# Graph attention, second layer: the output scaling and part of the weight sums on VectorE, the shift of a normalisation on ScalarE

## Chip, core and metric

One core of a Trainium2 chip runs the whole program. Its engines are TensorE (PE in the profile, with PEld for its weight loads), VectorE (DVE), ScalarE (ACT), GpSimd (POOL) and SyncE (SP, which only issues DMAs). The metric is the device time of one execution in microseconds (us), taken as the median of several executions. The profiled execution's "span" runs from its first to its last instruction.

## The reference, cut to what matters

Two layers over N = 4096 nodes of 512 features, with a residual and a normalisation after each. The change touches only the second:

```python
def _L1_gnn_ref(node_matrix, adjacency_matrix, Wks, Wqs, Wvs, Wo):
    eye = jnp.eye(n)
    adj = jnp.maximum(adjacency_matrix, eye)
    q = jnp.einsum('nd,hdk->hnk', node_matrix, Wqs)      # 8 heads of 64
    k = jnp.einsum('nd,hdk->hnk', node_matrix, Wks)
    v = jnp.einsum('nd,hdk->hnk', node_matrix, Wvs)
    scores = jnp.einsum('hqk,hmk->hqm', q, k) * kd ** (-0.5)
    scores = scores + IDENTITY_BIAS * eye - MASK_VAL * (1.0 - adj)
    att = jax.nn.softmax(scores, axis=-1)
    return jnp.einsum('hqm,hmk,hko->qo', att, v, Wo)

x = _layernorm(x + _L0_gnn_ref(x, adj, ...))
x = _layernorm(x + _L1_gnn_ref(x, adj, ...))
```

For each head and each query, the masked exponentials of 4096 scores are summed, multiplied with v, and divided by their sum.

## The kernel before

**Tiling of the second layer's attention.** Queries are cut into 8 groups g of 512 and heads into 4 couples m, which makes 32 pairs (g, m). For each pair the 4096 keys come in 32 blocks j of 128. One unit (g, m, j) is: `score`, four products of q and k on TensorE into a PSUM tile `s_ps` of 128 keys x (2 heads x 512 queries); the exponential in place on ScalarE (line 1559); the product with the mask on VectorE (line 1562), which reads `s_ps` and writes a tile `p` in SBUF, the weights; and `products`, four products of v and p on TensorE that are accumulated over j in `o_ps` (line 1614). There are three `s_ps` tiles, each used again as soon as line 1562 has read it, and 18 `p` tiles.

**Steps.** Three units make a step, so a pair has steps 0 to 9 with three units and a short step 10 with units 30 and 31. `step` (line 1727) writes this order into the queues: the scores of its units; in a short step also the sums and a projection for earlier pairs (below); the exponentials and masks; in a short step `close1` and `divide`; `add_up` for each unit; then the products of the step before; at the end `later.step()`. What is handed over with `later.at(k, ...)` in step s goes into the queues at the end of step s + k - 1, in the order in which it was handed over. Each engine then works through its own queue in that order, and each instruction waits for what it needs.

**The sums of the weights** (`add_up`, line 1566). The 32 weight tiles of a pair make 16 couples a, b (j = 2i and 2i + 1). Couple 0 starts `q_sum` on GpSimd (line 1578). Of the other fifteen, thirteen are first added into a by a DMA that accumulates (line 1595, issued by GpSimd) and then added to `q_sum` by GpSimd (line 1582). For two of them, i = 7 and i = 15, GpSimd adds both tiles to `q_sum`, without a DMA. The last pair has an order of its own for its couples 8 to 15; its couple 7 is like that of the others.

**The division** (`divide`, line 1636). In the short step of a pair, TensorE sums the `q_sum` of the pair before over partitions (line 1633). Reciprocals follow on VectorE (line 1656; one at the end of this short step, one at the end of the next pair's step 0), ScalarE copies them to all partitions (line 1648, into `r`), and at the end of step 4 `rest` (line 1650) multiplies the pair's output `o_sb` with `r` on GpSimd (line 1652), which gives `on`, the left operand of a later projection.

**The normalisation** (`close1`, line 1686). In the short steps from pair 5 on, one tile of 128 rows is projected with Wo (line 1678), added to the residual on VectorE (line 1689), and `normal_factors` (line 507) takes mean and variance on VectorE (lines 510 and 512) and then runs four instructions of one column on GpSimd: variance plus epsilon (514), power -1/2 (516), mean times this (518), times -1 (519). At the end of the next pair's step 2 ScalarE applies scale and shift (line 1694), and SyncE writes the rows out. The end of the last pair uses `factors` (line 1698), `shift` (1708) and `normalise` (1713), which split the same work between GpSimd and ScalarE.

Of the kernel before, what the change touches and what calls it, by code (L numbers as in the profile page):

```python
# [12 lines left out]
AF = mybir.ActivationFunctionType  # L13
ALU = mybir.AluOpType
# [415 lines left out]
def tile_gat_then_masked_attention(  # L430
# [16 lines left out]
    nc = tc.nc  # L447
# [59 lines left out]
    def normal_factors(y):  # L507

        st = small.tile([P, 6], F32, name="bn_st")
        nc.vector.bn_stats(st, y)  # L510
        mv = small.tile([P, 2], F32, name="bn_mv")
        nc.vector.bn_aggr(mv, st)
        ve = small.tile([P, 1], F32, name="bn_ve")
        nc.gpsimd.tensor_scalar(ve, mv[:, 1:2], EPS, None, op0=ALU.add)
        rs = small.tile([P, 1], F32, name="bn_rs")
        nc.gpsimd.tensor_tensor(rs, ve, minus_half, op=ALU.pow)
        nb = small.tile([P, 1], F32, name="bn_nb")
        nc.gpsimd.tensor_tensor(nb, mv[:, 0:1], rs, op=ALU.mult)
        nc.gpsimd.tensor_scalar(nb, nb, -1.0, None, op0=ALU.mult)
        return rs, nb  # L520
# [33 lines left out]
    later = Later()  # L554
# [18 lines left out]
    with tc.tile_pool(name="l0", bufs=NG) as l0, \  # L573
# [39 lines left out]
        def values(n, g):  # L613

            sup[n, g] = pools[n % 2][1].tile([P, GT, W0], F32, name="sup_t", bufs=NG)
            return sup[n, g]
# [34 lines left out]
        with tc.tile_pool(name="l0s", bufs=2) as sp:  # L651
# [32 lines left out]
            def factors(g, s4):  # L684

                t0, t1 = g * GT, (g + 1) * GT
                a = sp.tile([P, GT, H0], F32, name="aj")
                nc.scalar.activation(a, fs[g][:, 0], AF.Exp)
                dj[g] = l0.tile([P, GT, H0], F32, name="dj")
                nc.scalar.activation(dj[g], fs[g][:, 0], AF.Exp, scale=SLOPE - 1.0)  # L690
                fr = sp.tile([P, 2, H0, GT], F32, name="fr")
                src = fs[g][:, 1].rearrange("p t h -> p h t")
                nc.scalar.activation(fr[:, 0], src, AF.Copy)
                nc.scalar.activation(fr[:, 1], src, AF.Exp, scale=1.0 - SLOPE)
                flat = fs[g].rearrange("p k t h -> p k (t h)")
                nc.vector.tensor_reduce(span[:, g, 0:2], flat, AX.X, ALU.max)
                nc.vector.tensor_reduce(span[:, g, 2:4], flat, AX.X, ALU.min)
                s0 = values(0, g)
                nc.gpsimd.tensor_copy(s0[:, :, D0], a[:, :, 0])
                nc.gpsimd.tensor_copy(s4[:, 1:, :, D0], a[:, :, 1:].rearrange("p t h -> p h t"))  # L700
                for h in range(H0):
                    dst = s4[:, h] if h else s0
                    nc.gpsimd.tensor_tensor(dst[:, :, 0:D0], s4[:, h, :, 0:D0],
                                            a[:, :, h, None].to_broadcast([P, GT, D0]),
                                            op=ALU.mult)
                    nc.sync.dma_start(sup_d[h][:, t0:t1, :], dst)

                def rest():


                    n = 2 * H0 * GT
                    row = sp.tile([P, n], F32, name="fr_row")
                    nc.vector.transpose(row, fr.rearrange("p k h t -> p (k h t)"))
                    r0 = g * G % W
                    dst = fr_d[g * G // W][:, :, r0:r0 + G].rearrange(
                        "k h (t a r) -> a (k h) t r", a=NQ, r=SQ)
                    for q in range(NQ):
                        nc.sync.dma_start(dst[q], row[q * SQ:(q + 1) * SQ, :])
                if g + 1 < NG:
                    later.at(1, rest)  # L720
                else:
                    rest()
# [269 lines left out]
        with wait_by_tile("l0v", 2) as vp:  # L992
# [81 lines left out]
            def close(w, t):  # L1074
                i = w * WT + t
                y = agg_t[w][:, t].rearrange("p h d -> p (h d)")
                rs, nb = normal_factors(y)

                def normalise():
                    nc.scalar.activation(y, y, AF.Identity, bias=nb, scale=rs)  # L1080
                    nc.sync.dma_start(x1_d[i // GT][i % GT * P:(i % GT + 1) * P, :], y)
                later.at(5 if w + 1 < NW else 6, normalise)
# [22 lines left out]
    with wait_by_tile("l1", 1) as l1, wait_by_tile("l1a", 2) as lp, \  # L1105
# [3 lines left out]
        kt, vt, qt, at, mdt, pt, pw, q_sum, o_t, o_sb, on_t = ({} for _ in range(11))  # L1109
# [413 lines left out]
        with wait_by_tile("l1w", 2) as wp, wait_by_tile("l1o", 1, space=PSUM) as op:  # L1523
            NB = 3
            later = Later()
# [40 lines left out]
            def add_up(g, m, j):  # L1566

                if j % 2 == 0:  # L1570
                    return
                a, b = pt.pop((g, m, j - 1)), pt.pop((g, m, j))
                i, n = j // 2, NT // 2
                at_end = (g, m) == pairs[-1]

                def first():
                    q_sum[g, m] = wp.tile([P, HP, G], F32, name="q_sum")
                    nc.gpsimd.tensor_tensor(q_sum[g, m], a, b, op=ALU.add)

                def add(p):  # L1580
                    q = q_sum[g, m]
                    nc.gpsimd.tensor_tensor(q, q, p, op=ALU.add)  # L1582

                if i == 0:
                    later.at(1, first)
                elif at_end and i >= n - 5:
                    last_sum.extend((a, b))
                elif at_end and i >= n - 8:
                    later.at(2, lambda: nc.gpsimd.dma_start(a, b, accum_op=ALU.add))
                    in_pairs.append(a)  # L1590
                elif i % 8 == 7:
                    later.at(2, lambda: add(a))
                    later.at(3, lambda: add(b))
                else:
                    later.at(2, lambda: nc.gpsimd.dma_start(a, b, accum_op=ALU.add))  # L1595
                    later.at(5, lambda: add(a))
# [28 lines left out]
            def places():  # L1625

                return [(c, c // KD, slice(c // MA % 2 * GH, (c // MA % 2 + 1) * GH))
                        for c in range(0, P, MA)]
# [7 lines left out]
            def divide(g, m, s):  # L1636

                if m == 0:
                    on_t[g] = wp.tile([P, NP1, G], F32, name="on")
                n = index[g, m, 0] // NT  # L1640
                den = wp.tile([P, GH], F32, name="den_h", bufs=1)
                nc.scalar.activation(den, s[:, 0:GH], AF.Copy, accum_out=total[:, n:n + 1])
                rh = wp.tile([P, GH], F32, name="r_h", bufs=1)
                r = wp.tile([P, G], F32, name="r1", bufs=1)

                def spread(c, e, half):
                    for a in range(e * KD, (e + 1) * KD, MA):
                        nc.scalar.activation(r[a:a + MA, half], rh[c:c + MA, :], AF.Copy)  # L1648

                def rest():  # L1650
                    nc.scalar.activation(den, rh, AF.Copy, accum_out=most[:, n:n + 1])
                    nc.gpsimd.tensor_tensor(on_t[g][:, m, :], o_sb.pop((g, m)), r, op=ALU.mult)

                def invert(t):
                    a = slice(t * P, (t + 1) * P)
                    nc.vector.reciprocal(rh[:, a], den[:, a])

                for t in range(GH // P):
                    later.at(1 + t, lambda t=t: invert(t))
                for k, place in enumerate(places()):  # L1660
                    later.at(3 + k // 2, lambda place=place: spread(*place))
                later.at(6, rest)
# [23 lines left out]
            def close1(g, t, s, wait=4):  # L1686
                i = g * GT + t
                y = y_t.pop((g, t))
                nc.vector.tensor_tensor(y, y, s, op=ALU.add)

                rs, nb = normal_factors(y)

                def normalise():
                    nc.scalar.activation(y, y, AF.Identity, bias=nb, scale=rs)
                    nc.sync.dma_start(out[i * P:(i + 1) * P, :], y)
                later.at(wait, normalise)

            def factors(s):
                st = small.tile([P, 6], F32, name="bn_st")
# [8 lines left out]
            def shift(mv):  # L1708
                less = small.tile([P, 1], F32, name="bn_ve")
                nc.scalar.activation(less, mv[:, 0:1], AF.Copy, scale=-1.0)  # L1710
                return less
# [68 lines left out]
            y = y_t[tiles[-5]]  # L1780
# [16 lines left out]
            rs, nb = normal_factors(y)  # L1797
# [30 lines left out]
            mv, rs = by[3]  # L1828
# [41 lines left out]
```

## Time and profile before

| | |
|---|---|
| median of 3 runs (lowest, highest) | 3319.39 us (3316.53, 3320.89) |
| profiled execution, its own time | 3318.25 us |
| span of the profiled execution | 3316.3 us, granted clock 0.999 |
| VectorE busy, of the span | 2479.2 us (75%) |
| ScalarE busy | 1950.6 us (59%) |
| GpSimd busy | 2163.6 us (65%) |
| GpSimd busy from 2000 to 2200 us | 191.19 of 200 us |
| VectorE busy from 2000 to 2200 us | 138.29 of 200 us |
| ScalarE busy from 2000 to 2200 us | 121.31 of 200 us |
| weight additions of line 1582 on GpSimd | 535 records, 1367.4 us, 2556 ns each |
| scalings of line 1652 on GpSimd | 31, median 2258 ns |

The second layer's attention runs from about 1420 us to the end. A row of the timeline reads: start in us, length in us, engine, line, operation, names out<-in, shapes, number of instructions merged into the row, and in brackets the idle time of that engine just before it with what ended it. The length that the profile gives for an instruction on GpSimd can hold time in which it waited for an earlier one, or for a resource. Some records of a trace can be missing.

### The profile page before, as it was taken

How to read it: one execution, taken by the hardware profiler on the slowest of the kernel's cores; microseconds unless marked ns; L12 is line 12 of the kernel's file. 1: busy time of each engine (PE TensorE's matmuls, PEld its weight loads, DVE VectorE, ACT ScalarE, POOL GpSimd, SP SyncE). 2: the span in 40 equal slices, each digit the busy share in tenths (PEclk: the TensorE clock that was granted, in tenths of full speed). 3: DMA queues.
4: the chain of work that ended last, by engine and by line, in shares of the span. 5: the costliest groups of instructions: out<-in, count | busy, mean ns of one | idle time of the engine just before them, and what ended most of it. 6: DMA issues, size and time to landing. Idle time of an engine off the chain costs nothing.

```text
span 3316.3 us, 67188 instructions
## 1 busy us (share of the span) xinstructions
PE 3297.3 (99%) x27144; PEld 1963.8 (59%) x27144; DVE 2479.2 (75%) x3188; ACT 1950.6 (59%) x2449; POOL 2163.6 (65%) x1594
## 2 busy tenths in 40 slices
PE   9999999999999999999999999999999999999998
PEld 8899999999999777733333333333333333333333
DVE  6689899898999677467767666676766767666666
ACT  1367868878776310156656656566565656656554
POOL 6630040040030244389999999999999999999995
PEclk9999999999999999999999999999999999999999
DMA  8988796686532443499898988889889799898884
GB/s 191 230 198 189 212 189 169 150 182 147 138 93 59 109 147 120 163 217 207 192 211 222 229 196 193 210 189 256 205 192 212 189 209 251 190 211 193 203 204 116
DMA packets 398800, 612.04 MB, mean 185 GB/s; under 512 B 167632, under 2 KB 248528, under 8 KB 398480
## 3 DMA queue, kind: packets, MB, share of 16 engines
q0 software_dynamic: 97760, 259.55, 42.9%
q1 hardware_dynamic: 299280, 345.88, 33.6%
q8 instruction: 215, 3.52, 0.4%
q10 hardware_dynamic: 1440, 2.23, 0.3%
q14 instruction: 105, 0.86, 0.1%
HBM read 315.87 MB, written 109.25 MB: 128 GB/s over the span
## 4 chain that ended last, share of the span: by engine, by line
PE 94%; DMA 2%; POOL 2%; DVE 1%; issue 1%; ACT 0%; ACTq 0%; POOLq 0%; DVEq 0%
PE o_ps L1095 27%; PE o_ps L1614 25%; PE s_ps L1146 25%; PE o_ps L850 5%; PE s_ps L1678 3%; PE s_ps L1306 2%; PE s_ps L1256 2%; PE s_ps L1263 2%; DMA p<-p 2%; PE x_ps L1263 1%; PE x_ps L1256 1%; PE s_ps L1633 1%; POOL q_sum L1582 0%; PE s_ps L1302 0%; POOL p L1595 0%
## 5 line engine op out<-in xcount | busy, mean ns | idle before, releaser
L1582 POOL TENSOR_TENSOR q_sum<-q_sum,p 128x1024 f32<-128x1024 f32 x535 | 1367.4, 2556 | 65.2 <-DMA p<-p 39.8
L1562 DVE TENSOR_TENSOR p<-s_ps,adjT 128x1024 f32<-128x1024 f32 x896 | 1044.0, 1216 | 469.6 <-ACT s_ps L1559 439.2
L1559 ACT ACTIVATE s_ps<-s_ps 128x1024 f32<-128x1024 f32 x1021 | 967.2, 1007 | 597.7 <-PE s_ps L1146 597.5
L1146 PE MATMUL s_ps<-q_sb,k_sb 64*64 64x512 f32 x8192 | 943.5, 589 | 2.5 <-DVE p L1562 2.5
L1614 PE MATMUL o_ps<-p,v_sb 64*64 64x512 f32 x8192 | 943.9, 590 | 0.0
L1095 PE MATMUL o_ps<-sup_t,p 128*128 128x129 f32 x8192 | 915.5, 275 | 1.2 <-DVE p L646 1.2
L1095 PEld LDWEIGHTS o_ps<-sup_t,p 128*128 128x128 f32 x8192 | 915.1, 192 | 1.6 <-DVE p L646 1.4
L646 DVE SCALAR_TENSOR_TENSOR p<-fr_t,dj,az 128x1024 f32<-128x1024 f32 x512 | 650.0, 1284 | 65.7 <-PE o_ps L1095 36.8
L1146 PEld LDWEIGHTS s_ps<-q_sb,k_sb 64*64 64x64 f32 x8192 | 312.5, 133 | 569.5 <-issue 454.6
L1614 PEld LDWEIGHTS o_ps<-p,v_sb 64*64 64x64 f32 x8192 | 310.1, 133 | 570.8 <-issue 560.3
L630 ACT ACTIVATE z<-fr_t,f 128x1024 fp8e4<-128x1024 f32 x512 | 557.3, 1143 | 102.6 <-DVE az L641 102.3
L1595 POOL DMA_DIRECT2D p<-p x409 | 435.3, 1305 | 9.9 <-PE o_ps L1614 9.1
L1071 POOL DMA_DIRECT2D agg<-base_d x32 | 29.0, 1218 | 386.9 <-DMA sup_t<-sup_d 204.7
L591 POOL COPY seen<-token 128x1 f32<-128x1 f32 x24 | 10.9, 456 | 356.8 <-DVE token L589 356.8
L1562 DVE TENSOR_TENSOR p<-s_ps,md 128x1024 f32<-128x1024 f32 x128 | 150.7, 1217 | 67.0 <-ACT s_ps L1559 63.3
L641 DVE TENSOR_TENSOR az<-adjT,z 128x512 int32<-128x512 int32 x256 | 175.3, 685 | 3.3 <-ACT z L630 2.1
L606 ACT ACTIVATE adjT<-stage 128x1024 fp8e4<-128x1024 bf16 x128 | 130.9, 1052 | 16.8 <-DMA stage<-adj_d 16.8
L1678 PE MATMUL s_ps<-wo_sb,on 128*128 128x512 f32 x240 | 111.2, 605 | 0.0
L1648 ACT ACTIVATE r<-r_h 32x256 f32<-32x256 f32 x248 | 102.3, 412 | 2.9
L1057 ACT ACTIVATE agg<-o_ps,rinv 128x128 f32<-128x128 f32 x128 | 41.9, 369 | 70.1 <-DVE den L1050 48.8
L1330 ACT ACTIVATE v<-s_ps 128x256 f32<-128x256 f32 x28 | 10.7, 382 | 115.0 <-PE s_ps L1306 100.0
L1678 PEld LDWEIGHTS s_ps<-wo_sb,on 128*128 128x128 f32 x240 | 43.1, 189 | 56.6 <-issue 54.7
(295 smaller groups left out, 2236.5 us busy)
## 6 DMA issues: line engine op xcount, KB each, us to landing
p<-p POOLq DMA_DIRECT2D x412, 512.0 KB, 9.1
k_sb<-k_d SPq DMA_DIRECT2D x128, 512.0 KB
v_sb<-v_d SPq DMA_DIRECT2D x128, 512.0 KB
adj_d<-in_adj_dram POOLq DMA_DIRECT2D x32, 1024.0 KB, 11.1
sup_t<-sup_d SPq DMA_DIRECT2D x120, 258.0 KB
fr_t<-fr_d SPq DMA_DIRECT2D x16, 1024.0 KB
adjT_d<-adjT SPq DMA_DIRECT2D x32, 512.0 KB
adjT<-adjT_d SPq DMA_DIRECT2D x32, 512.0 KB
```

Source lines behind the costliest of these rows:

```text
L630: nc.scalar.activation(z[:, k, :], fr_t[w, h][:, 0, :], AF.Sign, bias=fs[j // GT][:, 0, (j + k) % GT, h:h + 1], saturate=False)
L641: nc.vector.tensor_tensor(az.bitcast(I32), adjT[w, j // CJ][:, j % CJ:j % CJ + 2, :].bitcast(I32), z.bitcast(I32), op=ALU.bitwise_and)
L646: nc.vector.scalar_tensor_tensor(p, fr[:, 1, :], dj[j // GT][:, j % GT, h:h + 1], az_t[w, h, j // 2][:, j % 2, :], op0=ALU.max, op1=ALU.mult)
L850: nc.tensor.matmul(out[:, t * HD:(t + 1) * HD], xb[:, c, t * P:(t + 1) * P], wb[:, c, :], start=not more and t == 0 and c == 0, stop=c == ...
L1095: nc.tensor.matmul(o[t // BK][:, t % BK, :], p[:, t * P:(t + 1) * P], s, start=(j == 0 and t % BK == 0), stop=(j == NT - 1), skip_group_ch ...
L1146: nc.tensor.matmul(s[c:c + MS, e, :], k[r, a + c:a + c + MS], qt[g, m][r, :], start=True, stop=True)
L1559: nc.scalar.activation(s, s, AF.Exp, scale=float(KD) ** -0.5)
L1562: nc.vector.tensor_tensor(p, s, keep[:, None, :].to_broadcast([P, HP, G]), op=ALU.mult)
L1582: nc.gpsimd.tensor_tensor(q, q, p, op=ALU.add)
L1595: later.at(2, lambda: nc.gpsimd.dma_start(a, b, accum_op=ALU.add))
L1614: nc.tensor.matmul(o[c, n, :], v[r, j % CH, c], p[r, e, :], start=(j == 0), stop=(j == NT - 1))
L1678: nc.tensor.matmul(s, on_t[g][:, m, t * P:(t + 1) * P], wo_sb[:, m, :], start=(m == 0 and not onto), stop=(m == NP1 - 1), skip_group_check ...
```

## The change

Three edits, all in the second layer's attention:

1. `add_up`: for the couples i = 7 and i = 15, b is added to a on VectorE, and GpSimd then adds a alone to `q_sum`. VectorE's addition is handed over for the step at whose end the first of GpSimd's two stood; the one that GpSimd keeps stands where its second was.
2. `rest` in `divide`: the product of `o_sb` and `r` goes from GpSimd to VectorE, at the same place.
3. `close1`: mean and variance by `factors` (two instructions of one column on GpSimd in place of four), and, when the tile is due, `shift` and `normalise` on ScalarE: minus the mean, this times the factor, and then the row-wise scale and shift, three instructions in place of one.

```diff
@@ add_up
                 elif i % 8 == 7:
-                    later.at(2, lambda: add(a))
-                    later.at(3, lambda: add(b))
+                    later.at(2, lambda: nc.vector.tensor_tensor(a, a, b, op=ALU.add))
+                    later.at(3, lambda: add(a))
@@ divide
                 def rest():
                     nc.scalar.activation(den, rh, AF.Copy, accum_out=most[:, n:n + 1])
-                    nc.gpsimd.tensor_tensor(on_t[g][:, m, :], o_sb.pop((g, m)), r, op=ALU.mult)
+                    nc.vector.tensor_tensor(on_t[g][:, m, :], o_sb.pop((g, m)), r, op=ALU.mult)
@@ close1
-                rs, nb = normal_factors(y)
-
-                def normalise():
-                    nc.scalar.activation(y, y, AF.Identity, bias=nb, scale=rs)
+                mv, rs = factors(y)
+
+                def close():
+                    normalise(y, y, shift(mv), rs)
                     nc.sync.dma_start(out[i * P:(i + 1) * P, :], y)
-                later.at(wait, normalise)
+                later.at(wait, close)
```

The functions that `close1` now calls stood in the kernel already:

```python
def factors(s):
    ...
    nc.gpsimd.tensor_scalar(rs, mv[:, 1:2], EPS, None, op0=ALU.add)
    nc.gpsimd.tensor_tensor(rs, rs, minus_half, op=ALU.pow)
    return mv, rs

def shift(mv):
    less = small.tile([P, 1], F32, name="bn_ve")
    nc.scalar.activation(less, mv[:, 0:1], AF.Copy, scale=-1.0)
    return less

def normalise(s, y, less, rs, meanwhile=None):
    nb = small.tile([P, 1], F32, name="bn_nb")
    nc.scalar.activation(nb, less, AF.Copy, scale=rs)
    ...
    nc.scalar.activation(y, s, AF.Identity, bias=nb, scale=rs)
```

In the queues of the changed kernel VectorE's new addition for i = 15 stands directly behind `o_sb` (line 1757) and the second reciprocal (line 1656) of the next pair's step 0, and in front of the three masks of its step 1. The one for i = 7 stands behind the masks of step 6, the scaling behind the masks of step 4. The order of TensorE's instructions is what it was.

## The prediction

> **What bounds the kernel now.** I read the page first, its part on busy times and the 40 slices.
>
> ```profile
> PE 3297.3 (99%) x27144; PEld 1963.8 (59%) x27144; DVE 2479.2 (75%) x3188; ACT 1950.6 (59%) x2449; POOL 2163.6 (65%) x1594
> ```
>
> TensorE is busy 99% of the span, at a granted clock of 0.999. A busy TensorE can still run below its pace, so next came TensorE's waits from 1400 us on, then the chain that ended last in order of time.
>
> ```profile
> PE s_ps L1146 <- DVE p L1562: 2.5, 4, 1.6
> ```
>
> ```profile
> 2325.33 0.57 PE s_ps L1633 x8
> 2325.90 3.63 PE s_ps L1678 x8
> ...
> 2384.63 0.57 PE s_ps L1633 x8
> ```
>
> The reader is to see a pace: one pair takes 59.30 us (2384.63 - 2325.33), and the timeline shows the same 59.29 to 59.30 for all pairs with a projection except three (59.89, 60.16, 59.71); of the pairs without one, three take 55.66 and one 57.45. The excess is 0.59 + 0.86 + 0.41 + 1.79 = 3.65 us. That is all a faster VectorE, ScalarE or GpSimd can win here: 0.11%. GpSimd's 95% (191 of 200 us) costs only this much. So what decides is whether the work that arrives on VectorE delays TensorE. Here the timeline of one pair's change to the next (short step, then steps 0, 1, 2):
>
> ```profile
> 2212.72 0.22 POOL L514 TENSOR_SCALAR bn_ve<-bn_mv 128x1 f32<-128x1 f32 x1 [1.16 <-DVE bn_mv L512]
> 2213.01 0.57 POOL L516 TENSOR_TENSOR bn_rs<-bn_ve,minus_half 128x1 f32<-128x1 f32 x1
> ...
> 2214.14 2.36 POOL L1582 TENSOR_TENSOR q_sum<-q_sum,p 128x1024 f32<-128x1024 f32 x1
> 2216.44 1.86 POOL L1595 DMA_DIRECT2D p<-p  x2
> 2217.66 7.93 POOL L1582 TENSOR_TENSOR q_sum<-q_sum,p 128x1024 f32<-128x1024 f32 x3
> ...
> 2219.12 0.68 DVE L1757 TENSOR_TENSOR o_sb<-o_sb,o_ps 128x512 f32<-128x512 f32 x1
> 2219.72 0.95 DVE L1656 RECIPROCAL r_h<-den_h 128x128 f32<-128x128 f32 x1
> 2220.58 3.42 DVE L1562 TENSOR_TENSOR p<-s_ps,adjT 128x1024 f32<-128x1024 f32 x3
> 2224.23 0.15 PEld L1146 LDWEIGHTS s_ps<-q_sb,k_sb 64*64 64x64 f32 x4 [0.28 <-DVE p L1562]
> ```
>
> VectorE has no idle time between 2219.12 and 2224.00 (2220.58 + 3.42): it is the late one. Its third mask ends at 2224.00 and the weight load that needs this `s_ps` tile (third unit of step 2) starts on schedule at 2224.23, so 0.23 us are left. How much later it may be is seen where VectorE once waited for a weight tile:
>
> ```profile
> 1956.77 1.90 PE L1146 MATMUL s_ps<-q_sb,k_sb 64*64 64x512 f32 x16
> 1957.76 2.46 DVE L1562 TENSOR_TENSOR p<-s_ps,adjT 128x1024 f32<-128x1024 f32 x2 [1.63 <-DMA p<-p]
> 1959.04 1.09 PE L1146 MATMUL s_ps<-q_sb,k_sb 64*64 64x512 f32 x8 [0.37 <-DVE p L1562]
> ```
>
> The third unit's load was due at 1958.06 (loads go every 0.43 us, one slot ahead of their products), came at 1959.04, 0.98 late, and the pair lost 0.59: 0.39 was absorbed. So a delay d of step 1's masks costs TensorE d - 0.23 - 0.39 = d - 0.62 us.
>
> [...] in the first layer:
>
> ```profile
> 36.24 5.13 POOL L883 TENSOR_TENSOR base<-base,bb 128x1024 f32<-128x1024 f32 x2
> 38.35 0.80 DVE L801 TENSOR_TENSOR p<-xT 128x512 f32<-128x512 f32 x1
> 39.19 2.74 DVE L803 TENSOR_TENSOR p<-p,xT 128x512 f32<-128x512 f32 x1
> ...
> 1189.41 2.35 POOL L1285 TENSOR_TENSOR k_sb<-k_sb,p 128x1024 f32<-128x1024 f32 x1 [6.36 <-DVE k_sb L1291]
> 1189.50 2.41 DVE L1215 TENSOR_TENSOR w_sk<-w_sk,adjT 128x128 f32<-128x128 f32 x1
> ```
>
> L803 usually takes 0.68 and L1215 0.28; here they end 0.6 and 0.15 after GpSimd does. L801 slipped in between two GpSimd instructions, L803 had to wait out the whole next one. The masks of line 1562 have one input in PSUM and show none of this (1216 ns beside a busy GpSimd). [...] the three additions from 2217.66 really begin when the two DMA issues are done (2218.30) and take 7.29/3 = 2.43 each.
>
> **The change part by part.**
>
> *GpSimd, removed per pair:* two additions (2 x 2.43), one scaling (2.26), two small instructions (0.57, from 2213.58 to 2214.14): 7.7 us. All of it lies beside TensorE, except the 3.65 us above, each of which follows a wait of VectorE for a weight tile that a late DMA or GpSimd held. I take all four as gone: -3.65.
>
> *ScalarE, added:* `shift` 0.19 and the factor 0.28 (rows of lines 1710 and 1715 at the end of the program), the row-wise part as before: about 0.5 us at the end of step 2. Step 3's exponentials, which start at most 0.15 late there now, start about 0.6 late; VectorE idles 1.8 us before step 3's masks. Cost nothing; without that cover at most 0.5 x 26 = 13 us.
>
> *Scaling on VectorE:* 0.68 us (two SBUF inputs, 128x512, as L801), behind step 4's masks, where VectorE idles 1.66 us and the third mask of the next step has about 0.74 + 0.39 to spare. A cover of 2.8 us: even behind a whole GpSimd addition (2.43 + 0.68) it costs 0.3. I take 0.
>
> *Addition for i = 7*, behind step 6's masks: 1.22 us (row of line 1602, two SBUF inputs, 1224 ns), same cover. It costs only if GpSimd has more than 1.6 us to go; bounds 0 and 0.85 per pair. I take 0, since GpSimd is then catching up between DMAs.
>
> *Addition for i = 15*, in front of step 1's masks: here is no cover. VectorE comes to it at 2220.58. Where is GpSimd? It is idle before line 514 (1.16 us), so its phase is tied to VectorE's mean, and what follows moves up by the 0.57 us of the two small instructions: addition to 2215.93, DMA issues to 2217.73, additions to 2220.16 and 2222.59. VectorE arrives 0.42 us after the second has begun, waits 2.0 us, adds 1.22, and the masks start 2222.59 + 1.15 - 2220.58 = 3.15 us late (1.15: two instructions in a row overlap by 0.07). Cost 3.15 - 0.62 = 2.53 us. What is queued behind it: three masks, for which the three score products of step 2 wait, and everything of TensorE behind these. Bounds: with no wait 1.15 - 0.62 = 0.53; with a whole addition to wait out 1.15 + 2.43 - 0.62 = 2.96.
>
> *Sum.* 26 changes with a normalisation (pairs 5 to 30): 26 x 2.53 = 65.8. Pairs 1 to 4, where nothing ties GpSimd: margin the same, wait taken as half an addition: 4 x 1.7 = 6.8. Pair 0 (no reciprocal) 1; the last pair, whose couple 7 meets a reciprocal, 1.5; its scaling ahead of the last sums on VectorE 0.5. Less 3.65: +72 us. The profiled execution is 1.1 us below the median, so 3319.4 + 72 = 3391 us.
>
> **Rivals.**
> 1. *The addition costs its own length only* (it slips in front of GpSimd's second addition, or does not block). For it: 0.42 us of phase is little, and a DMA issue that takes that much longer lets VectorE in first. Against: both phases hang on the same instruction, and pairs repeat to 0.02 us. Then 26 x 0.53 to 26 x 0.95, + 5, - 3.65: +15 to +26, about 3340 us.
> 2. *The other couple is exposed as well.* If GpSimd begins an addition just before VectorE reaches i = 7, 31 x up to 0.85 more, and the wait at i = 15 is a whole one: +84 to +110, about 3415 us. For it: fixed phases, all or nothing. Against: GpSimd has about 8 us of idle time per pair by then (2.6 now, 7.7 more, less its own waits behind VectorE), and by step 6 it waits for DMAs between additions.
> 3. *Not slower:* the relief of GpSimd decides. Place: weight tiles held by late DMAs in steps 6 to 9; price -3.65 us, so 3315.7. It decides if step 1's masks come less than 0.62 + 0.12 us late (3.65/31 = 0.12). For it: only GpSimd is near full. Against: 1.15 us of addition alone is more than 0.74.
>
> **How the numbers follow.** Chances: forecast 0.64 (3360 to 3412), rival 1 0.22 (3332 to 3350), rival 2 0.08, rival 3 0.06. Predicted 3391 us. The range 3338 to 3414 takes the forecast and most of rival 1 and leaves out most of rivals 2 and 3. Below 0.2% (6.6 us) this kernel cannot be told from unchanged: within it 0.05, nearly all of rival 3; faster 0.02, since only 3.65 us are there to be won; slower 0.93.
>
> **What would show it.** In the profile after: line 1592 on VectorE in two kinds, behind line 1656 lasting about 3.2 us with GpSimd's L1582 ending 1.2 us before it; TensorE waiting on `p` of L1562 once per pair in step 2; pairs of about 61.8 us; GpSimd busy near 170 of 200 us. A mean of 1.22 us for line 1592 there and pairs of 59.8 us are rival 1; pairs of 59.30 throughout are rival 3. I am wrong in the main step if masks of step 1 start late and TensorE does not wait.

## The result, and the profile after

| | before | after |
|---|---|---|
| median (lowest, highest), same chip | 3319.33 us (3316.53, 3320.89) | 3399.02 us (3393.62, 3401.53) |
| ratio, 95% interval | | 1.0238 [1.0228, 1.0248] |
| profiled execution: span, granted clock | 3316.3 us, 0.999 | 3397.5 us, 0.997 |

The change makes the kernel 79.7 us slower; 72 were forecast. The span grew by 81.2 us.

The page after, busy times:

```profile
PE 3330.9 (98%) x27144; PEld 1952.8 (57%) x27144; DVE 2667.4 (79%) x3282; ACT 1971.4 (58%) x2503; POOL 2007.8 (59%) x1446
```

GpSimd lost 156 us, VectorE gained 188, and TensorE has the same instructions as before. TensorE's waits from 1400 us on (line waited for, us in total, times, longest), and the busy times of a window in the middle (PE, PEld, DVE, ACT, POOL, then clock, DMA share, GB/s):

```profile
PE s_ps L1146 <- DVE p L1562: 44.8, 31, 1.7
```

```profile
2000.00:2200.00 200.00, 192.89 (x1704) 66.48 (x1700) 151.93 (x134) 122.19 (x167) 168.40 (x104) 1.00 0.80 187
```

The wait that stood at 2.5 us in 4 places has become 44.8 us in 31, about one for each change of pairs. GpSimd is at 168.4 of 200 us, from 191.2: relieved as planned, and to no use. These waits are 42.3 us more than before; TensorE's busy time is 33.6 us more (3330.9 - 3297.3) with as many instructions. The next view shows where most of both comes from.

The same stretch of a pair's change that the prediction read, now after (start, length, engine, line, operation):

```profile
2304.16 0.22 POOL L1704 TENSOR_SCALAR bn_rs<-bn_mv 128x1 f32<-128x1 f32 x1 [6.42 <-DVE bn_mv L1702]
...
2305.01 2.35 POOL L1582 TENSOR_TENSOR q_sum<-q_sum,p 128x1024 f32<-128x1024 f32 x1
...
2307.32 1.83 POOL L1595 DMA_DIRECT2D p<-p  x2
...
2308.52 5.47 POOL L1582 TENSOR_TENSOR q_sum<-q_sum,p 128x1024 f32<-128x1024 f32 x2
...
2310.56 0.68 DVE L1757 TENSOR_TENSOR o_sb<-o_sb,o_ps 128x512 f32<-128x512 f32 x1
2311.16 0.94 DVE L1656 RECIPROCAL r_h<-den_h 128x128 f32<-128x128 f32 x1
...
2312.02 3.05 DVE L1592 TENSOR_TENSOR p<-p,p 128x1024 f32<-128x1024 f32 x1
2313.95 3.33 POOL L1578 TENSOR_TENSOR q_sum<-p,p 128x1024 f32<-128x1024 f32 x1
2314.99 7.02 DVE L1562 TENSOR_TENSOR p<-s_ps,adjT 128x1024 f32<-128x1024 f32 x6
2316.26 3.35 PE L1146 MATMUL s_ps<-q_sb,k_sb 64*64 64x512 f32 x24 [1.70 <-DVE p L1562]
...
2317.39 0.21 PEld L1146 LDWEIGHTS s_ps<-q_sb,k_sb 64*64 64x64 f32 x8 [0.92 <-DVE p L1562]
...
2318.52 0.21 PEld L1146 LDWEIGHTS s_ps<-q_sb,k_sb 64*64 64x64 f32 x8 [0.93 <-DVE p L1562]
...
2319.43 2.75 PE L1614 MATMUL o_ps<-p,v_sb 64*64 64x512 f32 x24
```

Read it from GpSimd: the issues end at 2309.15 (2307.32 + 1.83), the two additions behind them at 2313.99. At 2.43 us each, the second began at 2311.56. VectorE came with line 1592 at 2312.02, 0.46 us too late, and ended 1.08 us after GpSimd's addition. So line 1592 lasts 3.05 us in place of 1.22, step 1's masks start 2.97 us late (2314.99 - 2312.02), and TensorE waits 1.70 us for the first of them. Its loads for the other two units then follow the masks, 1.13 us apart (2317.39, 2318.52), so that these 24 products last 3.35 us, where 24 others last 2.75. The 1.70 and the 0.60 make 2.30 of the 2.46 us that the pair loses. In turn line 1578 on GpSimd lasts 3.33 in place of 2.36: counted back from its end (2317.28), its 2.36 us began at 2314.92, near the end of VectorE's addition (2315.07).

In the groups of the window from 1400 us on (busy, mean ns, idle time before), line 1592 averages 2525 ns, more than twice its own length; GpSimd, by contrast, idles 161.9 us in sum ahead of the 31 normalisations:

```profile
L1592 DVE TENSOR_TENSOR p<-p,p 128x1024 f32<-128x1024 f32 x63 | 159.1, 2525 | 0.0
...
L1704 POOL TENSOR_SCALAR bn_rs<-bn_mv 128x1 f32<-128x1 f32 x31 | 6.9, 222 | 161.9 <-DVE bn_mv L1702 161.8
```

The starts of line 1633 give the period of each pair. Before: 59.30. After: 61.76 in most of the pairs with a projection, 62.4 to 62.6 in three, 63.9 in three, 61.92 in one and 60.07 in one. In the pair of 60.07, VectorE met GpSimd at another moment and the addition for couple 15 lasted 1.35 us.

The pairs of 63.9 have a cause of their own. The trace's record of TensorE's granted clock has it at one half from 2441.34, 2690.51 and 2939.69 us, for 3.413 us each time, and otherwise from 1400 us on only in the last 8 us; in the kernel before only in the last 7. The first two rows are the stretches of 3.41 us before and after the first of these moments; the other two lie around a stall whose clock stays whole (the first number behind the length is TensorE's busy time, the third from the right its clock):

```profile
2437.93:2441.34 3.41, 1.67 (x16) 0.41 (x16) 3.41 (x4) 0.74 (x2) 3.41 (x2) 1.00 0.43 123
2441.34:2444.75 3.41, 3.41 (x20) 1.00 (x16) 2.97 (x3) 2.06 (x3) 3.33 (x2) 0.50 0.02 5
2376.49:2379.90 3.41, 1.83 (x16) 0.42 (x16) 3.41 (x4) 0.74 (x2) 3.41 (x2) 1.00 0.32 93
2379.90:2383.31 3.41, 3.37 (x32) 1.13 (x32) 3.41 (x4) 3.01 (x6) 3.33 (x2) 1.00 0.02 5
```

The three moments lie 249.17 and 249.18 us apart, which is 73 times 3.413. In the run with couple 15 alone (below) they are 1879.64, 2251.69 and 2930.95: 372.05 and 679.26 us apart, 109 and 199 times 3.413. With both traces cut at these moments and at whole multiples of 3.413 us from them (from 1450 us to 20 us before the end), the stretches that come before a halving are, in the run with couple 15 alone, the three in which TensorE works least: 1.66, 1.67 and 1.69 us; the next has 1.70. In the kernel after they have about 1.67, 1.67 and 1.70, and two others, at 1.68 and 1.70, are not followed by a halving. So each of the six halvings comes behind a stretch in which TensorE worked 1.66 to 1.70 of 3.413 us; it comes in three pairs of 26, though TensorE waits 1.68 to 1.71 us at 25 of the 26 changes of pairs, and around the stall of the last two rows, where the stretch has 1.83 us of work, it does not. In run 7, where TensorE waits 0.92 us at a time, no stretch has less than 2.41, and the clock stays whole. This is a regularity of three traces; the cause of the halving was not shown.

In these three pairs couple 7 meets GpSimd as well, as in others:

```profile
2467.30 0.87 POOL L1595 DMA_DIRECT2D p<-p  x1 [0.69 <-PE o_ps L1614]
...
2467.91 8.40 POOL L1582 TENSOR_TENSOR q_sum<-q_sum,p 128x1024 f32<-128x1024 f32 x3
2467.97 3.67 DVE L1592 TENSOR_TENSOR p<-p,p 128x1024 f32<-128x1024 f32 x1
```

VectorE comes 0.20 us before the DMA issue ends (2468.17) and still waits out the first of the three additions behind it; run 8 comes back to this. Couple 7 lasts 3.5 to 3.75 us in 11 of 32 pairs and 1.2 to 2.7 in the others.

The sum of the prediction beside what the periods show (the normal periods taken, as there, as 59.30 and 55.66, so that the 3.65 us of before's late pairs are subtracted):

| term | forecast us | measured us |
|---|---|---|
| 26 changes of pairs, couple 15 | 65.8 | 64.0 (26 x 2.46) |
| further in these pairs | 0 | 7.0: clock 4.6 (3 x 1.52), couple 7 3.9 (six pairs at 0.61 to 0.79), other +0.2, the pair of 60.07 -1.7 |
| pairs 1 to 4 | 6.8 | 6.6 |
| up to the first line 1633 (pair 0) | 1 | 4.3 |
| the last pair and its end | 2 | 2.9 |
| before's late pairs | -3.65 | -3.65 |
| sum | 72 | 81.2 (span) |

The 4.3 us hold some scatter: in the run without either couple (below), where nothing ahead of that point is changed, the first line 1633 comes 1.8 us later than before. The share of 1.52 for a halved clock is from the run with couple 15 alone, where such pairs take 63.28.

### The profile page after: what moved, and what is told of

It reads as the page before. It is cut to its first block, busy times and chain, and to the rows that moved or that the text cites. A ratio compares the mean times of both kernels' runs of the same rounds, so it can differ in the third digit from the quotient of the medians.

```text
span 3397.5 us, 67150 instructions
## 1 busy us (share of the span) xinstructions
PE 3330.9 (98%) x27144; PEld 1952.8 (57%) x27144; DVE 2667.4 (79%) x3282; ACT 1971.4 (58%) x2503; POOL 2007.8 (59%) x1446
## 4 chain that ended last, share of the span: by engine, by line
PE 88%; DVE 6%; issue 4%; ACT 1%; POOL 0%; DMA 0%; DVEq 0%; ACTq 0%; POOLq 0%
PE o_ps L1095 27%; PE s_ps L1146 23%; PE o_ps L1614 22%; PE o_ps L850 5%; DVE p L1562 3%; PE s_ps L1678 3%; PE s_ps L1306 2%; PE s_ps L1256 2%; PE s_ps L1263 2%; PE x_ps L1263 1%; DVE p L1592 1%; ACT s_ps L1559 1%; PE x_ps L1256 1%; DVE o_sb L1757 1%; PE s_ps L1633 1%
## 5 line engine op out<-in xcount | busy, mean ns | idle before, releaser
L1562 DVE TENSOR_TENSOR p<-s_ps,adjT 128x1024 f32<-128x1024 f32 x896 | 1045.0, 1216 | 372.4 <-ACT s_ps L1559 359.6
L1582 POOL TENSOR_TENSOR q_sum<-q_sum,p 128x1024 f32<-128x1024 f32 x472 | 1208.5, 2560 | 85.4 <-DMA p<-p 66.4
L1146 PE MATMUL s_ps<-q_sb,k_sb 64*64 64x512 f32 x8192 | 968.8, 595 | 48.3 <-DVE p L1562 44.8
L1146 PEld LDWEIGHTS s_ps<-q_sb,k_sb 64*64 64x64 f32 x8192 | 300.3, 133 | 656.7 <-issue 393.3
L1595 POOL DMA_DIRECT2D p<-p x409 | 406.3, 1181 | 84.2 <-PE o_ps L1614 55.5
L1592 DVE TENSOR_TENSOR p<-p,p 128x1024 f32<-128x1024 f32 x63 | 159.1, 2525 | 0.0
L1704 POOL TENSOR_SCALAR bn_rs<-bn_mv 128x1 f32<-128x1 f32 x31 | 6.9, 222 | 161.9 <-DVE bn_mv L1702 161.8
L1578 POOL TENSOR_TENSOR q_sum<-p,p 128x1024 f32<-128x1024 f32 x32 | 100.0, 3124 | 0.0
```

What stands on the lines that cost most here:

```text
L1146: nc.tensor.matmul(s[c:c + MS, e, :], k[r, a + c:a + c + MS], qt[g, m][r, :], start=True, stop=True)
L1562: nc.vector.tensor_tensor(p, s, keep[:, None, :].to_broadcast([P, HP, G]), op=ALU.mult)
L1592: later.at(2, lambda: nc.vector.tensor_tensor(a, a, b, op=ALU.add))
```

## The experiments

Theory: the addition for couple 15, in front of step 1's masks, meets GpSimd's second addition, which shuts it out; everything else is small. Rivals: its own length or its place alone costs; the second couple costs; the relief of GpSimd or ScalarE's work counts. Each run was compared with the kernel before on the same chip.

### 1. Without the couples

The change with its first edit undone:

```diff
-                    later.at(2, lambda: nc.vector.tensor_tensor(a, a, b, op=ALU.add))
-                    later.at(3, lambda: add(a))
+                    later.at(2, lambda: add(a))
+                    later.at(3, lambda: add(b))
```

> The changed kernel with its first edit undone: both couples are added by GpSimd again; the scaling stays on VectorE and the shifts on ScalarE. Theory (the loss is VectorE's addition for couple 15, which waits for GpSimd's running addition and delays the masks of step 1): pairs of 59.30 us throughout, VectorE free of line 1592, about 3316 us (3314 to 3320), the time before less up to 3.65 us. Rival (the scaling and ScalarE's two more instructions carry part of the loss): 13 us from ScalarE (0.5 us times 26) and up to 0.3 us times 31 from the scaling, 3325 to 3340.

Measured: 3319.7 us, ratio 0.9998 [0.9989, 1.0007]. All pairs with a projection take 59.29 or 59.30; GpSimd is at 184.60 of the 200 us. So the scaling on VectorE and the three instructions on ScalarE cost nothing that can be measured, and the relief of GpSimd wins nothing: before's late pairs (0.59, 0.86 and 0.41) are gone, but two pairs without a projection take 57.44 and 57.09 where before had one of 57.45, 1.42 more in sum.

### 2. Couple 7 alone

```diff
+                elif i == 15:
+                    later.at(2, lambda: add(a))
+                    later.at(3, lambda: add(b))
                 elif i % 8 == 7:
```

> The changed kernel with couple 15 given back to GpSimd; couple 7 stays on VectorE. Theory: the pairs' common excess of 2.46 us goes; what stays is what couple 7 costs where it has to wait long, in the changed kernel's trace the excess over 61.76 us of some pairs (0.65, 0.79, 2.15, 2.15, 2.13, 0.63: 8.5 us): 3316 to 3326 us. Rival (each couple on VectorE costs about half): about 3355 us.

Measured: 3323.13 us, ratio 1.0009 [1.0001, 1.0018]. Couple 7's addition (minimum, median, maximum in ns; the line number has moved by three):

```profile
L1595 DVE TENSOR_TENSOR p<-p,p x32: 1211/1392/3617, 1436.7 to 3266.0; 128x1024 f32<-128x1024 f32 x32
```

Thirteen of 32 last more than 2.9 us; in the pairs with a projection where it does, the pair takes 59.57 to 60.03. The cost is there, but it is 3 us by the medians and 4.5 by these pairs' periods, so couple 7 is not the main part.

### 3. More work for GpSimd

The changed kernel with edit 3 undone: GpSimd has its four small instructions again. If the meeting decides, the phase of GpSimd does, and 0.57 us more work should help.

```diff
-                mv, rs = factors(y)
-                def close():
-                    normalise(y, y, shift(mv), rs)
+                rs, nb = normal_factors(y)
+                def normalise():
+                    nc.scalar.activation(y, y, AF.Identity, bias=nb, scale=rs)
```

> The changed kernel with its third edit undone, so that GpSimd again runs two small instructions (0.57 us) between the power and its next addition. Theory [...]: in the changed kernel GpSimd's second addition begins 0.47 us before VectorE comes to the addition for couple 15; 0.57 us later it begins about 0.1 us after it, VectorE goes first, line 1592 behind line 1656 lasts 1.2 to 1.6 us instead of 3.05, pairs take 59.9 to 60.3 us, 3335 to 3350 us, though GpSimd has more to do. Rival (it is the length of VectorE's queue at this place, or GpSimd's load): as the changed kernel or slower, 3395 to 3405 us.

Measured: 3346.83 us, ratio 1.0081 [1.0065, 1.0098], 52 us less than the changed kernel. Its timeline at a change of pairs:

```profile
2288.28 1.86 POOL L1595 DMA_DIRECT2D p<-p  x2
2289.49 6.36 POOL L1582 TENSOR_TENSOR q_sum<-q_sum,p 128x1024 f32<-128x1024 f32 x2
...
2291.54 0.94 DVE L1656 RECIPROCAL r_h<-den_h 128x128 f32<-128x128 f32 x1
2292.40 1.22 DVE L1592 TENSOR_TENSOR p<-p,p 128x1024 f32<-128x1024 f32 x1
2293.55 7.02 DVE L1562 TENSOR_TENSOR p<-s_ps,adjT 128x1024 f32<-128x1024 f32 x6
```

The issues end at 2290.14, so GpSimd's first addition ends at about 2292.5 and its second would begin there. VectorE is there at 2292.40, slips in, and lasts 1.22. GpSimd pays instead: its two additions take until 2295.85, so that the second began at about 2293.49 (2295.85 - 2.36), near the end of VectorE's (2293.62). Pairs take 59.93. This is the strongest evidence for the theory: the same work on VectorE, more on GpSimd, and 1.83 us less per pair. Edit 3 takes ScalarE's two short instructions away as well, but they are no rival: run 1 keeps them with pairs of 59.30, run 4 with pairs of 59.86.

### 4. The same length with one input

Couple 15's addition replaced by a maximum over a alone, of nearly the same length, at the same place. The weights of b are left out of the sum.

```diff
-                    later.at(2, lambda: nc.vector.tensor_tensor(a, a, b, op=ALU.add))
+                    later.at(2, lambda: nc.vector.tensor_reduce(junk, a, AX.X, ALU.max))
                     later.at(3, lambda: add(a))
```

> The changed kernel, where for couple 15 VectorE takes the maximum of tile a over 1024 columns into a small tile that nobody reads (one input in SBUF, about the same length) instead of adding b to a. The weights of b (one block of 128 keys in 32) are so left out of the sums; GpSimd's queue is that of the changed kernel. Theory [...]: about 1.2 us at this place, masks of step 1 late by 1.15, TensorE loses 0.5 us per pair: 3333 to 3345 us. Rival (any VectorE instruction of that length here costs what the addition costs): 3390 to 3400 us.

Measured: 3339.8 us, ratio 1.006 [1.0043, 1.0077].

```profile
L1593 DVE TENSOR_REDUCE junk<-p x31: 1156/1158/1210, 1460.7 to 3247.8; 128x2 f32<-128x1024 f32 x31
```

No one of the 31 is held up, in a place where the addition waited 1.83 us in 25 of 26 pairs. Pairs take 59.86. The maximum also writes much less than the addition, but the masks of line 1562, which have one input in SBUF and write as much as the addition, take 1216 ns on average beside the same GpSimd. So here the wait goes with the second input in SBUF (3.05 us with two, 1.16 and 1.22 with one), and TensorE loses 0.56 for a delay of 1.08.

### 5. The moved addition

Couple 15's addition behind the masks of step 3, where VectorE idles before the next masks; the other edits as in the change.

```diff
+                elif i == 15:
+                    later.at(5, lambda: nc.vector.tensor_tensor(a, a, b, op=ALU.add))
+                    later.at(6, lambda: add(a))
                 elif i % 8 == 7:
```

> The changed kernel with VectorE's addition for couple 15 handed over three steps later, so that it stands behind the masks of step 3 (and GpSimd's addition of a behind those of step 4). Theory [...]: there VectorE idles about 1.7 us and GpSimd is then issuing its DMAs and not adding, so that line 1592 lasts 1.2 us and nothing is delayed: pairs of 59.3 us but for couple 7, 3316 to 3326 us, with the same number of instructions on every engine. Rival (VectorE has too much to do, wherever it stands): 3335 us or more.

Measured: 3351.91 us, ratio 1.0096 [1.0081, 1.0111]: a miss by 26 us. The moved addition itself lasts 1.22, but the two others now do not: the scaling lasts 3.8 to 3.9 us in 19 of 31 pairs, and couple 7 has a median of 4140 ns. Most pairs take 60.9 to 61.0, and 59.29 where neither waits longer than about 1 us.

### 6 and 7. Half the length, and twice

As in run 4, with a maximum over 512 columns, and with the one over 1024 twice in a row (b is left out again).

```diff
-                    later.at(2, lambda: nc.vector.tensor_reduce(junk, a, AX.X, ALU.max))
+                    later.at(2, lambda: nc.vector.tensor_reduce(junk[:, 0:1], a[:, 0:1, :], AX.X, ALU.max))
```

> As the run with one input, with a maximum over 512 of the 1024 columns. The weights of b are left out of the sums again. Theory (a delay d of step 1's masks costs d less about 0.5 us): d is about 0.55, pairs of 59.30 to 59.40 us, 3318 to 3328 us. Rival (every instruction at this place costs its own length): pairs of 59.85, 3335 us.

> As the run with one input, with the maximum over 1024 columns taken twice. The weights of b are left out of the sums again. Theory: d is about 2.15 us, pairs of 59.30 + 2.15 - 0.5 = 60.95 us, about 3338 + 31 x 1.07 = 3371 us. Rival (the loss saturates, because TensorE has other work to do): below 3355 us.

Measured, one execution each: 3321.33 us with pairs of 59.33 to 59.34, and 3372.86 us with pairs of 60.99. Both as expected. With run 4 and the changed kernel they give a line: delays of about 0.55, 1.08, 2.2 and 2.97 us cost 0.04, 0.56, 1.69 and 2.46 per pair. That is the delay less 0.5.

### 8. Moved, and couple 7 on GpSimd

```diff
+                elif i == 7:
+                    later.at(2, lambda: add(a))
+                    later.at(3, lambda: add(b))
```

> As the run with the addition moved behind step 3, with couple 7 given back to GpSimd: the version that the theory takes for the best. Theory: pairs of 59.30 us throughout and the stalls of the kernel before mostly gone, 3314 to 3320 us, so equal to the kernel before or at most 0.15% faster. Rival (GpSimd's relief is worth nothing and the extra addition costs something): 3321 to 3326 us.

Measured: 3334.59 us, ratio 1.0045 [1.0031, 1.0059]: again a miss. The scaling (line 1655 here) lasts 3.8 to 3.9 in most pairs, and such pairs take 60.3, the others 59.30:

```profile
2360.44 1.22 DVE L1592 TENSOR_TENSOR p<-p,p 128x1024 f32<-128x1024 f32 x1
2361.57 3.48 DVE L1562 TENSOR_TENSOR p<-s_ps,adjT 128x1024 f32<-128x1024 f32 x3
2361.81 2.36 POOL L1582 TENSOR_TENSOR q_sum<-q_sum,p 128x1024 f32<-128x1024 f32 x1 [1.08 <-DVE p L1592]
2364.13 1.75 POOL L1598 DMA_DIRECT2D p<-p  x2
...
2364.97 3.86 DVE L1655 TENSOR_TENSOR on<-o_sb,r 128x512 f32<-128x512 f32 x1
2365.29 5.76 POOL L1582 TENSOR_TENSOR q_sum<-q_sum,p 128x1024 f32<-128x1024 f32 x2
```

GpSimd's addition of a now waits for VectorE's (1.08 us idle in the brackets), which ties GpSimd's phase to VectorE's: two DMA issues, then additions, just when VectorE comes with the scaling. The issues end at 2365.88, and the scaling lasts until 2368.83, past the first addition behind them. In eight other pairs it starts just as soon behind the start of the two issues and lasts about 0.7:

```profile
2185.22 1.74 POOL L1598 DMA_DIRECT2D p<-p  x2
...
2186.04 0.69 DVE L1655 TENSOR_TENSOR on<-o_sb,r 128x512 f32<-128x512 f32 x1
...
2186.55 2.80 POOL L1582 TENSOR_TENSOR q_sum<-q_sum,p 128x1024 f32<-128x1024 f32 x1
```

This one is done while GpSimd still issues (until 2186.96), so the issue alone did not hold VectorE up here. What tells the pairs apart is in the trace's record of the semaphores: when the weight tile landed that GpSimd's next addition waits for. From the fifth scaling on, the 18 long ones start 0.10 to 0.15 us after this landing. Of the eight short ones five start 0.07 to 1.05 us before it, two have another instruction of GpSimd (line 1125) in front of the addition, and the last has no addition close behind it. Run 5 divides in the same way. So in these 18 pairs the addition whose tile was there went ahead of VectorE. No run moved the landing, so this is a regularity and not a cause shown; for couple 7 it has exceptions (in the kernel after, the addition at 2653.97 lasts 1.22 us, 0.20 us after the landing).

### 9. Moved, all else on GpSimd

Run 8 with the scaling on GpSimd as well (line 1655, `nc.vector` to `nc.gpsimd`), to see whether its wait was all of run 8's loss.

> As the run before it with the moved couple 15 (VectorE's addition behind step 3, couple 7 on GpSimd), and the scaling on GpSimd again; of the change only the moved couple 15 and the ScalarE part are left. Theory (the 3.86 us scalings, behind which step 5's masks are late, are all of that run's extra 15 us): line 1592 lasts 1.22 us, no pair takes 60.3, pairs 59.30, 3314 to 3321 us. Rival (the moved addition itself costs, through GpSimd's addition that waits for it and the weight tiles that come late behind that): pairs of 59.6 to 60.4 remain, 3326 to 3336 us.

Measured: 3327.13 us, ratio 1.0025 [1.0014, 1.0035]; pairs of 59.73 to 59.79. The rival has the numbers, but not the mechanism:

```profile
2055.57 2.27 POOL L1655 TENSOR_TENSOR on<-o_sb,r 128x512 f32<-128x512 f32 x1
...
2056.24 2.68 DVE L1592 TENSOR_TENSOR p<-p,p 128x1024 f32<-128x1024 f32 x1
...
2058.84 7.09 DVE L1562 TENSOR_TENSOR p<-s_ps,adjT 128x1024 f32<-128x1024 f32 x6
```

The moved addition now meets the scaling itself, which runs on GpSimd until 2057.84, and ends 1.08 us after it. In run 8 each pair with a long scaling took 60.3 us and each other one 59.30, so that its loss goes with the scaling on VectorE. Put back on GpSimd, the scaling stands in the way from the other side, and about half of the loss stays (the two intervals just overlap).

### 10. Couple 15 alone, in its place

The change with couple 7 on GpSimd (the diff of run 8).

> The change with couple 7 on GpSimd again; couple 15 and the scaling stay on VectorE. Theory (couple 15 is the loss; couple 7 and its meeting with the scaling gave the pairs of 62.4 and 63.9 us): line 1592 lasts about 3.0 us, pairs 61.75 with few or none above 62, 3384 to 3392 us, some 7 to 15 us under the changed kernel. Rival (the phase of GpSimd at couple 15 depends on couple 7's being gone from it as well): line 1592 lasts 1.2 us, pairs 59.9, about 3340 us.

Measured: 3390.74 us, ratio 1.0219 [1.0203, 1.0234].

```profile
L1595 DVE TENSOR_TENSOR p<-p,p x31: 1162/3051/3275, 1460.3 to 3295.6; 128x1024 f32<-128x1024 f32 x31
```

Pairs take 61.76, three 63.28 (each with 3.4 us of halved clock in it and without couple 7, to which the theory had put down the pairs of 63.9), one 59.87 and one 60.06. Couple 7 thus makes 8 us of the changed kernel's time by the medians; the intervals of the two ratios overlap, so that this size is rough.

## Why the prediction was right, and where its sizes were off

- *TensorE's pace of 59.30 us, and that VectorE at the change of pairs decides*: right. Run 1 holds 59.30 in all pairs with a projection.
- *What is absorbed, 0.62 us*: 0.50 to 0.52 in runs 4 and 7 and in the kernel after. One late pair had been read; it gave 0.1 too much.
- *Couple 15 shut out by GpSimd's second addition*: shown by runs 3 and 4. VectorE came 0.46 us after that addition began (0.42 in the forecast), the masks were 2.97 late (3.15) and the pair lost 2.46 (2.53). That it takes two inputs in SBUF was an estimate of the forecast, from rows of the first layer (line 803, 2.74 us in place of 0.68); run 4 bears it out here (1.16 us with one). The 0.18 less in the delay and the 0.11 less absorbed nearly cancel; that is luck.
- *Pairs 1 to 4 at 6.8 us*: 6.6 measured, by luck too. Couple 15 waits 0.46 us there (line 1592 lasts 1.68), not half an addition. The pair without a long couple 7 loses 1.17 us, the three with one (3.61 to 3.68) lose 1.81 to 1.83: about 4.7 us are couple 15's and 1.9 couple 7's.
- *The 0.57 us of two small instructions set GpSimd's phase*: right, and it decides 52 of the 80 us (run 3). Edit 3, which looks free, is what turns couple 15 from 0.63 into 2.46 us per pair.
- *Scaling and ScalarE at nothing*: right where they stand without the couples (run 1). In the kernel after, the first four scalings last 2.97 us, and so do those of the three slow-clocked pairs. Run 10 has the same, there in the pairs of 63.28; in the first of them step 3 of TensorE starts 25.32 us after the sums (line 1636 in that run) in place of 23.90, so that 1.42 of the 1.52 us are lost ten us before the scaling begins. It follows from the slow stretch and is nearly hidden.
- *Couple 7 at nothing*: the mis-sized term. The bound of 0.85 for a whole addition to wait out was right (0.61 to 0.79 measured), the value in it was not: "GpSimd is then catching up between DMAs" holds in two pairs of three only. By the periods it is 3.9 us in the pairs with a projection, about 1.9 in pairs 1 to 4, and an unknown part of what the head lost; 8 us by the medians of the kernel after and run 10.
- *The clock*: missing from the sum, 4.6 us. It stood at one half for 3.413 us three times, each behind a stretch of that length in which TensorE worked 1.67 to 1.70 us; why it did so there, and not behind the other 1.70 us waits, was not shown.
- *The relief, -3.65*: it did not come. In run 1 the late pairs with a projection are gone (1.86 us), but two without one came (1.42 us more than before), and the median is the same. In the sum it serves only as the line that the periods are counted from.
- *Rivals*: rival 1's price (pairs of 59.83 to 60.25) is what runs 3 and 4 show, where VectorE comes before GpSimd's second addition (pairs of 59.93) or does not wait for it (59.86). Rival 2 is true in part: couple 7 is exposed in 11 of 32 pairs. Rival 3 fails: its point was a delay below 0.74 us.

No version here is faster than the kernel before. What runs 5, 8 and 9 leave open is a place where none of the two-input operations meets GpSimd; with 3.65 us to win at most, none was looked for.

## What to carry to other kernels

Ask of an operation that moves to VectorE not only what it lasts but whether it has two inputs in SBUF, and what GpSimd does at that moment: here that made 3.05 us of 1.22, where an operation with one input lasted 1.21 at most (run 4), and the price at the change of pairs was the whole delay less half a microsecond. Two engines of which one waits out the other's addition, and which are tied to the same events, met here in the same way round after round (in 25 changes of 26), so that a shift of 0.57 us was worth 52 us, 1.5% of the time; and moving one operation moved later meetings too (the scaling went from 0.68 to 3.86 us in 18 pairs of run 8). Relief of an engine that does not set the pace bought nothing here (run 1).

## What was not expected

- More work on GpSimd, 0.57 us per pair, made the kernel 52 us faster (run 3).
- Between two of GpSimd's additions that stand back to back in its queue, VectorE came about 0.1 us ahead of the second one, went first, and lasted 1.22 us (run 3).
- Behind DMA issues it did not go first: a scaling of 0.68 us lasted 3.86, with the rest of the issues (0.91) and one addition (2.43) to wait out, in all 18 pairs of run 8, from the fifth scaling on, where the addition's tile had landed before and no other instruction stood between.
- TensorE's granted clock stood at one half for 3.41 us in 3 pairs of 26 (kernel after and run 10 alike), at 1.5 us each, behind stretches of that length with 1.66 to 1.70 us of TensorE's work; in each of the two traces the moments lie whole multiples of 3.413 us apart.
- A one-input maximum of 128x1024 beside a busy GpSimd lasted 1158 ns (median of 31) and never more than 1210 (run 4).
